# Where the list products of a graph-attention layer stand in TensorE's order, and when its last masks are loaded

## The chip, the core and the metric

The program runs on one core of a Trainium2 chip, in one launch. A core has five engines with an instruction queue each: PE (TensorE, matrix products), DVE (VectorE), ACT (ScalarE), POOL (GpSimd, here the issuer of gathers) and SP (SyncE, the issuer of most other transfers). All transfers are moved by the core's 16 DMA engines. The metric is the device time of the launch in microseconds (us).

## What is computed

Four layers over one graph of N = 2708 nodes with D = 512 features. Each layer is `x = layernorm(x + layer(x, adj))`. Layers 0, 1 and 3 multiply the adjacency with features and the features with weights. The change lies in layer 2, which holds two attention sub-layers one after the other:

```
def _gat_layer(x, W, adj):
    proj = x @ W
    Wh, Ws = jnp.split(proj, 2, axis=-1)
    scores = Wh @ Ws.T
    a = jax.nn.softmax(scores, axis=-1) * adj
    out = a @ Wh
    out = out + x
    return jax.nn.leaky_relu(out, NEG_SLOPE)
```

The softmax runs over all 2708 scores of a row before the adjacency masks them. The adjacency is sparse (about 0.6% of its entries are set), and the kernel uses that: the product `a @ Wh` is not made densely, but over lists of the neighbours that a block of 128 nodes has.

## The kernel before

**Chunks and walks.** The rows of the score matrix are split into six chunks of 512, 512, 512, 512, 384 and 276 columns (`CH`; chunk 0 to 5). The scores are kept transposed, so a chunk is 22 tiles (`NB`) of 128 nodes by the chunk's width. `Attention.layer` runs over the chunks. In *walk* k PE computes the scores of chunk k: products into `spx`, `spy` and `sp`, for the chunks of 384 columns and more in a form with seven products instead of eight on half tiles. ACT copies them out of PSUM, and DVE keeps the running maximum `top`.

**Softening.** In the same walk k DVE and ACT *soften* chunk k-1 (`soften`, called by `layer` between the steps of the walk): subtract the shift, exponentiate (ACT), add to the sum, multiply with the mask `a` of the adjacency, and store the tile to a DRAM table `pairs`, by SP. Beside each row of softened scores the table holds the row of features `Wh` (stored earlier from `z`). The masks are loaded in six groups of up to four tiles (`load_mask`, by SP): groups 0 and 1 at the walk's first two steps, group g+2 when the softening comes to group g. The last chunk is softened after the last walk.

**Lists.** When a chunk has been softened, POOL gathers rows of `pairs` by index lists (`fetch`, rows `g<-pairs,givers`), each 128 rows into a tile of a ring of 11 (`WIDES`). PE multiplies a gathered tile's scores with its features (`weigh`, rows `acc<-g`). For each block of 128 nodes there are 12 gathers: four lists that are full 128x128 products and eight quarter lists, 128x32, issued four together. A chunk of 512 columns has 48 gathers, the sixth has 27; both sub-layers together have 510. The lists of chunk k are gathered and multiplied from walk k+2 on; what is left when the walks end follows in the *tail*.

**The order of the work.** No scheduler reorders: `issue` (L71) records every instruction with a dependency on the one before it on its engine, so each engine runs in the order in which Python issues, and every row of the profile carries L71. Where list products stand among PE's products is decided at build time by a clock of the kernel's own, `self.clock`, which is advanced by what the issued products should take (`cost`). A gather is given a time (`fetch`): it begins when the one before it is done, takes 1.15 us, and its tile is taken as there 6 us later; for the first gather of a chunk the begin is put at the clock + 16. `weigh` issues the next list product if its tile is there by that clock, and returns False if not. `fetch_ahead` issues gathers up to 10 ahead (`AHEAD`) of the products. `layer` calls `weigh` up to three times after each step ("end") of a walk; at a step's middle ("mid") it only softens. With `wait=True` the product is issued whatever the clock says.

**The tail.** After the walks the softening of the last chunk and the remaining lists are mixed with other PE work that a generator, `fill`, hands out step by step: for the first sub-layer `second` (the mixing and projection of the second), for the second sub-layer `early`, the first products of layer 3 (`acc<-m,xh` and `acc<-m,xl`). `early` needs normalized rows of the attention's result, and calls `need`, which issues list products with `wait=True` until those rows are made: all of chunk 3 and one block and four lists of chunk 4.

A walk's stretch of the second sub-layer is named by W and its number; W5 is the start of walk 5 there, 1888.9 us.

Of the kernel before, what the change touches and what calls it, by code (L numbers as in the profile page):

```python
# [22 lines left out]
NB = 22  # L23
NP = NB * P
DC = D // P
# [24 lines left out]
def rows_of(i):  # L50
    return min(P, N - i * P)
# [434 lines left out]


STREAMED = 4
SOFT = NB + 2 * 2
ALONE = 18  # L490
SEVEN = [k for k in range(len(CH)) if CH[k][1] >= 384]
# [884 lines left out]
class Chunk:  # L1376


    def __init__(self, ly, k):
        self.ly, self.k, self.cw = ly, k, CH[k][1]  # L1380
        self.name = f"{ly.number}_{k}"
        self.blocks = blocks_of(k)
        self.s, self.masks, self.ends = {}, {}, []
        self.half = self.cw // 2
        self.seven = k in SEVEN
        self.part, self.complete, self.ready, self.top = {}, [], [], None
        self.softened = 0
        self.apart = 2 if self.seven else 1
        self.fetched, self.rden = [], None
        self.x, self.first = {}, {}  # L1390
        self.rows = set()
        self.mv = None

        self.to_weigh = []
        for q, (i, _, _) in enumerate(self.blocks):
            ts = lists_of(i)
            self.to_weigh += [(q, t, t is ts[0], t is ts[-1]) for t in ts]
        self.to_fetch = [(q, t) for q, ts, _, _ in self.to_weigh for t in ts]
        self.first_fetch = self.to_fetch[0]
# [9 lines left out]
class Attention:  # L1409
# [7 lines left out]
    def __init__(self, fast):  # L1417
        self.f, self.k, self.nc = fast, fast.k, fast.nc
        self.page, self.bank = fast.page, fast.bank
        tc = self.k.tc  # L1420
        self.scratch = self.k.ctx.enter_context(
            tc.tile_pool(name="pairs", bufs=1, space=DRAM)
        )

        self.pairs = [
            [
                self.scratch.tile([NP, 2 * PAIR + D], FP, tag=f"p{a}{b}", name=f"pairs{a}{b}")
                for b in range(2)  # L1430
            ]
            for a in range(2)
        ]
        self.mixed = self.scratch.tile([DC, P, D], FP, tag="mixed", name="mixed")
        self.quarter = [
            [
                self.scratch.tile(
                    [2, P, pairs_of(k)[0] * P], FP, tag=f"q{a}_{k}", name=f"quarter{a}_{k}"
                )
                for k in range(len(CH))  # L1440
            ]
            for a in range(2)
        ]
        self.sums = [
            [
                self.scratch.tile([3, P, 2, 2 * P], FP, tag=f"u{a}_{k}", name=f"sums{a}_{k}")
                for k in range(STREAMED)
            ]
            for a in range(2)
        ]  # L1450
        self.layers = [AttentionLayer(a, self.pairs[a]) for a in range(2)]
        self.clock, self.fetch_free, self.pending = 0.0, 0.0, []
        self.left = None


    def blank(self):
# [140 lines left out]
    def sum_weights(self, ly, k):  # L1597
# [6 lines left out]
        names = ("s1", "s2", "s4")  # L1604
        if k < STREAMED:
            ly.streamed[k] = [self.page(f"{n}_{a}_{k}", FP, (P, 2, wide)) for n in names]
# [273 lines left out]
    def soften(self, ch):  # L1880


        nc, v, cw = self.nc, ch.softened, ch.cw
        ch.softened += 1
        if v < NB:
            n = rows_of(v)
            s = ch.s[v][:n, :cw]
            nc.vector.tensor_sub(s, s, ch.shift[:n, :cw])
        j = v - ch.apart
        if 0 <= j < NB:  # L1890
            s = ch.s[j][: rows_of(j), :cw]
            nc.scalar.activation(s, s, AF.Exp)
        j -= ch.apart
        if j < 0:
            return
        if j == NB - 1:
            ch.softened = SOFT
        if j == 0 and ch.k >= 2:
            while self.chunks[ch.k - 2].to_fetch:
                self.weigh(True)  # L1900
        if j % DC == 0 and j + 2 * DC < NB:
            self.load_mask(ch, j // DC + 2)
        n = rows_of(j)
        s = ch.s[j][:n, :cw]
        if j == 0:
            ch.sum = self.page(f"sum{ch.name}")
            nc.vector.tensor_copy(ch.sum[:, :cw], s)
        else:
            nc.vector.tensor_add(ch.sum[:n, :cw], ch.sum[:n, :cw], s)
        nc.vector.tensor_mul(s, s, ch.masks.pop(j)[:n, :cw])  # L1910
        to = ch.ly.pairs[ch.k % 2][j * P : j * P + n, :]
        if cw == BANK:
            nc.sync.dma_start(
                to[:, : 2 * PAIR].rearrange("j (r x) -> j r x", x=PAIR)[:, :, D:],
                ch.s[j][:n, :].rearrange("j (r x) -> j r x", x=2 * P),
            )
            return
        for r in range(2):
            w = min(2 * P, cw - r * 2 * P)
            nc.sync.dma_start(  # L1920
                to[:, r * PAIR + D : r * PAIR + D + w],
                ch.s[j][:n, r * 2 * P : r * 2 * P + w],
            )
# [17 lines left out]
    def fetch(self, ch):  # L1941


        q, t = ch.to_fetch.pop(0)
        g = self.f.wide(f"g{ch.name}_{q}_{t}")
        i, _, w = ch.blocks[q]

        for b in (q, q + 1):
            self.load_rows(ch, b)

        h = t // ONLY if t < QUARTERS * ONLY else (QUARTERS - 1, 0)[q % 2]
        first, width = (D + P + h * QW, D + P - h * QW) if q % 2 else (0, D + (h + 1) * QW)
        self.nc.gpsimd.indirect_dma_start(
            out=g[:, :width],
            out_offset=None,
            in_=ch.ly.pairs[ch.k % 2][:, :],
            in_offset=bass.IndirectOffsetOnAxis(ap=self.k.givers[:, i, t : t + 1], axis=0),
            element_offset=(q // 2) * PAIR + first,
        )

        begin = max(self.fetch_free, self.clock + (16 if (q, t) == ch.first_fetch else 0))
        self.fetch_free = begin + 1.15
        ch.fetched.append((g, self.fetch_free + 6))

# [28 lines left out]
    def weigh(self, wait=False):  # L1993

        nc = self.nc
        self.fetch_ahead()
        ch = next((c for c in self.chunks if c.to_weigh), None)
        if ch is None:
            return False
        q, ts, first, last = ch.to_weigh[0]  # L2000
        if len(ch.fetched) < len(ts):
            return False
        if ch.fetched[len(ts) - 1][1] > self.clock and not wait:
            return False
        ch.to_weigh.pop(0)
        if ch.rden is None:
            self.divisor(ch)
        w = ch.blocks[q][2]
        gs = [ch.fetched.pop(0)[0] for _ in ts]
        if first:  # L2010
            ch.acc = self.bank(1, f"acc{ch.name}_{q}")
            if ch.ly.number == 1:
                ch.first[q] = self.page(f"x1{ch.name}_{q}")
                self.nc.sync.dma_start(ch.first[q][:w], self.k.saved[1][ch.blocks[q][0]][:w])
        for h, g in enumerate(gs):
            lo, m = (0, w) if len(gs) == 1 else (h * QW, QW)
            e, z = (0, P - lo) if q % 2 else (D + lo, 0)
            nc.tensor.matmul(
                ch.acc[lo : lo + m],
                g[:, e : e + m],  # L2020
                g[:, z : z + D],
                start=first,
                stop=last,
            )
        self.advance(cost(D) if len(gs) == 1 else 1.1)
        if last:
            a = (ch, q, ch.acc, ch.x.pop(q), ch.first.pop(q, None))
            self.later(1.5, lambda: self.end(*a))
        self.fetch_ahead()
        return True  # L2030
# [86 lines left out]
    def layer(self, ly, chunks, fill):  # L2117
        f = self.f
        self.chunks, self.made = chunks, {}
        for k, ch in enumerate(chunks):  # L2120
            old = chunks[k - 1] if k else None
            following = chunks[k + 1] if k + 1 < len(chunks) else None

            n = -1
            for what in self.walk(ch):
                if what == "mid":
                    if old and n >= 3 and old.softened < SOFT:
                        self.soften(old)
                    continue
                n += 1  # L2130
                if old and n < 2:
                    self.load_mask(old, n)
                    self.greatest(old, last=n == 1)
                if old and n >= 4:
                    for _ in range(n % 2 == 0 if ch.seven else 1 + n % 2):
# [15 lines left out]
                        self.restore(ly, i)  # L2151
                self.greatest(ch)

                for _ in range(3):
                    if not self.weigh():
                        break
                if old and n == 2:
                    self.shift_rows(old)
                if old and n == 3:
                    self.shift_columns(old)  # L2160
            assert not old or old.softened == SOFT
        last = chunks[-1]
        self.load_mask(last, 0)
        self.load_mask(last, 1)
        self.greatest(last, last=True)
        self.until(self.clock + 3, fill)
        self.shift_rows(last)
# [119 lines left out]
```

## Time and profile before

| what | us |
| --- | --- |
| median of three runs | 2363.23 (2360.31 to 2371.82) |
| the profiled execution | 2341.13 |
| its span (first to last instruction) | 2339.0, mean granted clock 0.985 |

The windows of the profile, cut by stage, for the attention layer: the stage's length, the busy time of the engines in it, PE's granted clock, and the share of time in which the DMA engines are busy.

| stage (us from the span's start) | length | PE | DVE | POOL | clock | DMA |
| --- | --- | --- | --- | --- | --- | --- |
| sub-layer 0, walk 2 (900 to 1000) | 100 | 92.0 | 79.5 | 51.2 | 0.95 | 0.82 |
| walk 3 (1000 to 1105) | 105 | 99.9 | 81.6 | 49.5 | 0.98 | 0.79 |
| walk 4 (1105 to 1184) | 79 | 74.7 | 65.7 | 40.7 | 0.96 | 0.84 |
| walk 5 (1184 to 1247) | 63 | 61.9 | 52.2 | 39.2 | 1.00 | 0.98 |
| tail (1247 to 1467) | 220 | 214.2 | 69.5 | 84.1 | 0.98 | 0.96 |
| sub-layer 1, walk 2 (1605 to 1710) | 105 | 97.5 | 90.0 | 53.2 | 0.97 | 0.81 |
| walk 3 (1710 to 1813) | 103 | 95.1 | 86.2 | 50.7 | 0.98 | 0.81 |
| walk 4 (1813 to 1889) | 76 | 69.8 | 68.0 | 44.0 | 1.00 | 0.90 |
| walk 5 (1889 to 1949) | 60 | 58.6 | 51.2 | 36.3 | 1.00 | 0.90 |
| tail up to the last forced list (1949 to 2026) | 77 | 52.3 | 32.1 | 41.1 | 0.87 | 0.84 |
| the rest, with layer 3 (2026 to 2339) | 313 | 298.8 | 132.8 | 61.4 | 0.99 | 0.41 |

How to read it: a stage in which PE's busy time falls short of its length holds waits of PE. A clock below 1.00 means that PE ran part of the stage at half speed; that time counts as busy. POOL's busy time is that of issuing gathers. The rows quoted further on have the start, the length, the engine, the line, the operation, output and inputs, the count, and in brackets the idle time of the engine just before with what ended it ("issue": nothing that the profile shows).

### The profile page before, as it was taken

What the parts mean: (1) busy time and instruction counts of PE and PEld (TensorE: products, weight loads), DVE (VectorE), ACT (ScalarE), POOL (GpSimd) and SP (SyncE); (2) the same over time, 40 slices, a digit from 0 to 9 for tenths busy, and PEclk for the clock granted to TensorE, in tenths of its full rate; (3) what the DMA queues carried; (4) which work ended last, traced back from release to release, by engine and by line L of the source; (5) the groups of instructions that cost most, each with busy time, mean ns of one, the idle gap of its engine ahead of it and who ended that gap; (6) DMA issues with size and microseconds to landing.
All of it is one profiled execution on the core that took longest, in us unless ns stands there. A gap on an engine that the chain in (4) does not pass through costs nothing.

```text
span 2339.0 us, 29486 instructions
## 1 busy us (share of the span) xinstructions
PE 2237.2 (96%) x9724; PEld 1515.8 (65%) x9724; DVE 1547.5 (66%) x3180; ACT 725.9 (31%) x1654; POOL 717.8 (31%) x827
## 2 busy tenths in 40 slices
PE   9999999999999998999999999998998997899997
PEld 6776876777545786566764345787565763466685
DVE  6777787777655679778784512579888896354523
ACT  7444452222111243233332101243233332251221
POOL 2433521111000002635566450002634564643000
PEclk9999999999999999999999999999999998999999
DMA  9966752223576426968899998426978899884311
GB/s 346 283 186 189 205 148 76 79 77 115 194 262 253 157 77 205 335 218 318 293 362 360 341 399 333 169 78 210 330 243 286 307 306 343 265 249 148 110 47 42
DMA packets 285139, 523.27 MB, mean 224 GB/s; under 512 B 42926, under 2 KB 134758, under 8 KB 284976
## 3 DMA queue, kind: packets, MB, share of 16 engines
q1 hardware_dynamic: 216320, 306.34, 37.9%
q0 software_dynamic: 68656, 214.96, 27.6%
q8 instruction: 78, 1.28, 0.2%
q14 instruction: 85, 0.70, 0.1%
HBM read 335.34 MB, written 185.83 MB: 223 GB/s over the span
## 4 chain that ended last, share of the span: by engine, by line
PE 71%; DVE 13%; issue 6%; DMA 6%; ACT 2%; POOL 1%; SPq 1%; another core or an unknown queue 0%; DVEq 0%; ACTq 0%; POOLq 0%
PE acc L71 27%; PE spx L71 10%; PE mm L71 8%; PE spy L71 8%; PE z L71 6%; PE wst L71 6%; DVE s L71 5%; PE sp L71 3%; DVE sum L71 2%; DMA at<-in_adj_t 1%; DVE top L71 1%; DMA g<-pairs,givers 1%; DMA x<-in_x 1%; DMA x<-x 1%; DVE r L71 1%
## 5 line engine op out<-in xcount | busy, mean ns | idle before, releaser
L71 POOL DMA_INDIRECT g<-pairs,givers x510 | 535.8, 1051 | 912.5 <-issue 359.3
L71 PE MATMUL acc<-m,xh 128*128 128x512 f32 (+4 forms) x1584 | 566.1, 379 | 8.4 <-issue 7.0
L71 PE MATMUL acc<-m,xl 128*128 128x512 f32 (+4 forms) x1584 | 549.5, 365 | 11.0 <-DVE xl L71 9.4
L71 PEld LDWEIGHTS acc<-m,xh 128*128 128x128 f32 (+1 forms) x1584 | 288.1, 188 | 71.9 <-issue 28.6
L71 PEld LDWEIGHTS acc<-m,xl 128*128 128x128 f32 (+1 forms) x1584 | 288.3, 188 | 54.7 <-DVE xl L71 10.4
L71 PE MATMUL acc<-g 128*32 128x512 f32 (+1 forms) x1020 | 285.0, 610 | 12.2 <-DMA g<-pairs,givers 7.5
L71 PE MATMUL mm<-w,ht 128*128 128x512 f32 (+1 forms) x528 | 223.3, 593 | 0.0
L71 ACT CAST m<-at 128x512 fp32r<-128x512 uint8 (+5 forms) x396 | 199.1, 567 | 40.2 <-DMA at<-mask 20.1
L71 PE MATMUL spx<-xs,wst_sb 128*128 128x256 f32 (+1 forms) x800 | 201.3, 375 | 9.2 <-DVE s L71 9.1
L71 PEld LDWEIGHTS spx<-xs,wst_sb 128*128 128x128 f32 x800 | 149.3, 193 | 47.2 <-issue 14.8
L71 DVE TENSOR_TENSOR s<-s,shift 128x512 f32<-128x512 f32 (+3 forms) x264 | 162.4, 619 | 24.7 <-ACT shift L71 14.4
L71 ACT ACTIVATE s<-s 128x512 f32<-128x512 f32 (+3 forms) x264 | 152.0, 582 | 84.8 <-DVE s L71 74.7
L71 DVE TENSOR_TENSOR s<-s,a 128x512 f32<-128x512 f32 (+3 forms) x264 | 166.0, 629 | 18.5 <-issue 9.5
L71 PEld LDWEIGHTS acc<-g 128*32 128x32 f32 (+1 forms) x1020 | 79.7, 136 | 148.5 <-issue 107.4
L71 PEld LDWEIGHTS mm<-w,ht 128*128 128x128 f32 (+1 forms) x528 | 95.8, 186 | 116.6 <-issue 112.3
L71 ACT COPY s<-spx 128x256 f32<-128x256 f32 (+1 forms) x300 | 106.0, 361 | 196.0 <-PE spx L71 143.5
L71 DVE TENSOR_TENSOR sum<-sum,s 128x512 f32<-128x512 f32 (+4 forms) x252 | 156.3, 620 | 4.1 <-ACT s L71 4.1
L71 DVE TENSOR_TENSOR top<-top,s 128x512 f32<-128x512 f32 (+4 forms) x240 | 149.6, 623 | 13.7 <-ACT s L71 9.6
L71 PE MATMUL z<-w,xt 128*128 128x512 f32 (+1 forms) x352 | 151.4, 596 | 0.0
L71 PE MATMUL wst<-xt,mixed 128*128 128x512 f32 (+2 forms) x384 | 150.9, 545 | 0.0
L71 PE MATMUL spy<-xs,wst_sb 128*128 128x256 f32 (+1 forms) x480 | 121.9, 377 | 9.4 <-DVE s L71 9.2
L71 PE MATMUL sp<-xs,wst_sb 128*128 128x276 f32 (+5 forms) x512 | 129.1, 460 | 0.0
(190 smaller groups left out, 2686.3 us busy)
## 6 DMA issues: line engine op xcount, KB each, us to landing
pairs<-z_sb SPq DMA_DIRECT2D x84, 768.0 KB
pairs<-s SPq DMA_DIRECT2D x168, 256.0 KB
s<-sums SPq DMA_DIRECT2D x96, 256.0 KB
at<-in_adj_t SPq DMA_DIRECT2D x84, 256.0 KB
xres<-x POOLq DMA_DIRECT2D x44, 256.0 KB
x<-o POOLq DMA_DIRECT2D x43, 256.0 KB
pairs<-s SPq DMA_DIRECT2D x84, 128.0 KB
a<-mask SPq DMA_DIRECT2D x40, 256.0 KB
```

Of the source, the lines that this page charges most:

```text
L71: ins = call(*args, **kw)
```

## The change

Five edits, all of order; what is computed stays the same.

- `FIRST_LANDS`: the build-time clock puts the first gather of a chunk at the clock + 5 instead of + 16.
- `SPACING`: in walks 2, 3 and 4 a list product is issued only once the clock has reached `next_list`, which then moves on by 1.2 or 1.1 us per list (from no earlier than the clock - 4). In these walks `weigh` is called up to two times after a step instead of three.
- `weigh` is also called once at every "mid" of a walk, in all walks.
- `masks_ahead`: for chunks 4 and 5 five mask groups are loaded ahead of the softening instead of two; those of chunk 4 at the first five steps of walk 5.
- The first masks of chunk 5 (five groups) are loaded at the last five steps of walk 5, and no longer (two groups) after it.

The ring, `AHEAD` and the instructions stay as they are. In the order of the instructions as built, list products of chunks 0 and 1 begin earlier in their walks; all 48 of chunk 2 stand in walk 4 (before: 32 there and 16 in walk 5); 40 of chunk 3 stand in walk 5 (before: 20); and in the tail of the second sub-layer some 26 lists follow walk 5 up to what `early` needs (before: 44), and the lists of chunk 5 stand earlier among the products of layer 3.

```diff
--- before.py
+++ after.py
@@ -486,6 +486,8 @@
 
 
 STREAMED = 4
+FIRST_LANDS = 5
+SPACING = {2: 1.2, 3: 1.2, 4: 1.1}
 SOFT = NB + 2 * 2
 ALONE = 18
 SEVEN = [k for k in range(len(CH)) if CH[k][1] >= 384]
@@ -1385,6 +1387,7 @@
         self.seven = k in SEVEN
         self.part, self.complete, self.ready, self.top = {}, [], [], None
         self.softened = 0
+        self.masks_ahead = 2 if k < STREAMED else 5
         self.apart = 2 if self.seven else 1
         self.fetched, self.rden = [], None
         self.x, self.first = {}, {}
@@ -1451,6 +1454,7 @@
         self.layers = [AttentionLayer(a, self.pairs[a]) for a in range(2)]
         self.clock, self.fetch_free, self.pending = 0.0, 0.0, []
         self.left = None
+        self.spacing, self.next_list = 0.0, 0.0
 
 
     def blank(self):
@@ -1898,8 +1902,8 @@
         if j == 0 and ch.k >= 2:
             while self.chunks[ch.k - 2].to_fetch:
                 self.weigh(True)
-        if j % DC == 0 and j + 2 * DC < NB:
-            self.load_mask(ch, j // DC + 2)
+        if j % DC == 0 and j + ch.masks_ahead * DC < NB:
+            self.load_mask(ch, j // DC + ch.masks_ahead)
         n = rows_of(j)
         s = ch.s[j][:n, :cw]
         if j == 0:
@@ -1958,7 +1962,7 @@
             element_offset=(q // 2) * PAIR + first,
         )
 
-        begin = max(self.fetch_free, self.clock + (16 if (q, t) == ch.first_fetch else 0))
+        begin = max(self.fetch_free, self.clock + (FIRST_LANDS if (q, t) == ch.first_fetch else 0))
         self.fetch_free = begin + 1.15
         ch.fetched.append((g, self.fetch_free + 6))
 
@@ -2002,6 +2006,10 @@
             return False
         if ch.fetched[len(ts) - 1][1] > self.clock and not wait:
             return False
+        if self.spacing and not wait:
+            if self.clock < self.next_list:
+                return False
+            self.next_list = max(self.next_list, self.clock - 4) + self.spacing * len(ts)
         ch.to_weigh.pop(0)
         if ch.rden is None:
             self.divisor(ch)
@@ -2122,14 +2130,19 @@
             following = chunks[k + 1] if k + 1 < len(chunks) else None
 
             n = -1
+            self.spacing = SPACING.get(k, 0.0)
             for what in self.walk(ch):
                 if what == "mid":
                     if old and n >= 3 and old.softened < SOFT:
                         self.soften(old)
+                    self.weigh()
                     continue
                 n += 1
+                if old and n < old.masks_ahead:
+                    self.load_mask(old, n)
+                if not following and n > NB - 1 - ch.masks_ahead:
+                    self.load_mask(ch, n - NB + ch.masks_ahead)
                 if old and n < 2:
-                    self.load_mask(old, n)
                     self.greatest(old, last=n == 1)
                 if old and n >= 4:
                     for _ in range(n % 2 == 0 if ch.seven else 1 + n % 2):
@@ -2151,7 +2164,7 @@
                         self.restore(ly, i)
                 self.greatest(ch)
 
-                for _ in range(3):
+                for _ in range(2 if self.spacing else 3):
                     if not self.weigh():
                         break
                 if old and n == 2:
@@ -2159,9 +2172,8 @@
                 if old and n == 3:
                     self.shift_columns(old)
             assert not old or old.softened == SOFT
+        self.spacing = 0.0
         last = chunks[-1]
-        self.load_mask(last, 0)
-        self.load_mask(last, 1)
         self.greatest(last, last=True)
         self.until(self.clock + 3, fill)
         self.shift_rows(last)
```

## A prediction, made from the kernel before

> **What bounds the kernel now.** I read the page first, then the chain of waits, the windows of the second attention sub-layer's end, and its timelines by engine.
>
> ```profile
> span 2339.0 us, 29486 instructions
> PE 2237.2 (96%) x9724; PEld 1515.8 (65%) x9724; DVE 1547.5 (66%) x3180; ACT 725.9 (31%) x1654; POOL 717.8 (31%) x827
> PE 71%; DVE 13%; issue 6%; DMA 6%; ACT 2%; POOL 1%; SPq 1%; another core or an unknown queue 0%; DVEq 0%; ACTq 0%; POOLq 0%
> L71 POOL DMA_INDIRECT g<-pairs,givers x510 | 535.8, 1051 | 912.5 <-issue 359.3
> L71 PE MATMUL acc<-g 128*32 128x512 f32 (+1 forms) x1020 | 285.0, 610 | 12.2 <-DMA g<-pairs,givers 7.5
> ```
>
> PE bounds the program: 96% busy, and most of the chain is its own work. No instruction is taken away, so a gain can only come from PE's 102 idle us, from time in which it is busy but slowed by its clock, and from list products that run poorly. The 7.5 us put down to gathers understate the last: a product that waits for its gather piece by piece counts as busy.
>
> ```profile
> 1920.00:1960.00 40.00, 30.73 (x130) 19.54 (x128) 30.46 (x68) 17.50 (x41) 22.64 (x20) 0.91 0.91 325
> 1960.00:2000.00 40.00, 31.26 (x92) 12.17 (x93) 17.97 (x36) 5.90 (x10) 18.41 (x20) 0.87 0.88 315
> 2000.00:2040.00 40.00, 33.34 (x102) 16.58 (x101) 13.74 (x29) 7.68 (x15) 26.11 (x24) 0.96 0.79 252
> ```
>
> In these windows (busy us and counts of PE, PEld, DVE, ACT, POOL, then clock, DMA share, GB/s) PE loses 25 of 120 us and its clock falls to 0.87: the worst stretch of the program. The timeline says why:
>
> ```profile
> 1940.66 0.32 SPq L71 DMA_DIRECT2D a<-mask  x1
> 1953.34 0.56 DVE L71 TENSOR_TENSOR s<-s,a 128x384 f32<-128x384 f32 x1 [7.50 <-issue]
> 1956.91 0.80 PE L71 MATMUL acc<-m,xh 128*128 128x512 f32 x1 [6.97 <-issue]
> 1966.94 0.79 PE L71 MATMUL acc<-m,xl 128*128 128x512 f32 x1 [9.24 <-DVE xl L71]
> 1975.59 0.95 POOL L71 DMA_INDIRECT g<-pairs,givers  x1 [18.99 <-PE acc L71]
> ...
> 1981.32 5.48 PE L71 MATMUL acc<-g 128*32 128x512 f32 x14
> ...
> 2018.94 1.05 PE L71 MATMUL acc<-g 128*32 128x512 f32 x2 [2.37 <-DMA g<-pairs,givers]
> 2020.85 5.39 PE L71 MATMUL acc<-g 128*128 128x512 f32 x8 [0.86 <-DMA g<-pairs,givers]
> 2025.67 0.79 PE L71 MATMUL acc<-m,xh 128*128 128x512 f32 x1
> ```
>
> A mask load of chunk 4 was issued 12.6 us before its multiplication could start; DVE stood 7.5 us. Behind it in DVE's queue were the rest of that softening and the `xl` splits, so PE idled 6.97 and 9.24 us; POOL, whose ring of 11 tiles empties only when PE multiplies, stood 18.99 us. Then 36 lists came as one burst, 1981.32 to 2025.67: 44.4 us, at POOL's pace of 0.95 + 0.30 = 1.26 us a gather. I call 2025.67 the marker; walk 5 (the scores of the last chunk) began at 1888.9, so the marker is W5+136.8.
>
> **What the Trainium skill says.** "TensorE: Matmul & The Clock Gate", Part 1, What's actually happening: after an idle window of some 3.4 us PE runs at half clock until a busy window has passed. The trace agrees: 17.1 us at 0.5 from 1953.1, 3.4 to 6.8 us after most gaps. An idle of 3 us costs about 1.7 us more. The same page, Part 2, Step-by-step: matmuls stay in program order, only weight loads are pulled ahead. So a list product ordered ahead of its gather's landing blocks all scores behind it; the burst shows it. "DMA: Bandwidth & Descriptors", Issuing engines are not separate DMA queues: SP's and POOL's transfers interleave on the same 16 DMA engines. The trace has these 79 to 91% busy in the windows above, and gathers landing 4 to 6 us after issue, a mask after 12.6. So denser gathers may land later.
>
> **The change part by part.** PE, DVE, ACT, POOL and SP have the same instructions in both programs as built; only order moves. I lay PE's changed order over the times of before.
>
> *Masks five groups ahead.* Chunk 4's loads leave their places between SP's stores of `s` (each 0.45 to 0.5 us of issue) for the start of walk 5; chunk 5's are issued in walk 5 too. Five loads ahead of SP's stores delay these by 5 x 0.35, under 2 us, at a time when stores of chunk 4 have not begun. The 7.5 us on DVE go. PE's 16.2 us do not go whole: the softening of chunk 4 is late next, and `xl` stands behind it. I leave PE 5 us there: -11 us, clock windows apart.
>
> *Lists of chunk 2 all in walk 4.* Before, 32 of 48 were there and 16 in walk 5, so the first gather of chunk 3 came at 1901.5 (W5+12.6). Now it can come by about W5+4. The 16 lists cost walk 4 what they leave walk 5: 16 x 0.47 = 7.5 us (12 lists that are ready take 4 x 0.87 + 2 x 1.07 = 5.6 us, or 0.47 each). No gain by itself.
>
> *Lists of chunk 3 and the end of sub-layer 1.* The spread over "mid" points puts 40 instead of 20 of chunk 3's lists into walk 5, so POOL's ring empties there and its 18.99 us stop goes; the burst shrinks from 36 to some 26 lists. From walk 5's start to the marker POOL must issue 48 + 16 = 64 gathers. At 1.28 to 1.4 us (what it does while unblocked and in practice) that is 82 to 90 us; with the start at W5+4 and a landing of 6 us the marker is W5+92 to W5+100. PE's own work in the stretch (136.8 less 16.2 of idle, about 9 of half clock, and the burst's 44.4 against 36 x 0.47 = 17) gives 84; less the 7.5 moved to walk 4 still leaves gathers as the limit. I take W5+96: 136.8 - 96 = 41 us earlier, less 7.5 paid in walk 4: **-33 us**; the mask's 11 are within it, since POOL was stopped at the same time. Bounds -15 (pace 1.6) and -40.
>
> *Lists of chunk 5.* `FIRST_LANDS` 5 instead of 16 makes the build clock believe in an early landing. Before, its first list product came at marker + 74.6 (2100.3) with the gathers from 2080.5. In the changed order it stands after 19 groups of 1.82 us and 20 lists at 0.47, marker + 44, while DVE's softening of chunk 5 (2041.3 to 2068.2), 44 stores on SP and the landing come to marker + 50 when eight softening steps go ahead of the `xl` wait of 7.07 us. PE would stand about 6 us; bounds 0 and 14: **+6 us**.
>
> *Walks 2 to 4 of both sub-layers.* Their PE gaps over 0.3 us sum to 17 us in sub-layer 0 and 14 in sub-layer 1; half-clock windows add (20.4 + 10.2)/2 = 15. Two of them:
>
> ```profile
> 910.82 1.13 PE L71 MATMUL spx<-xs,wst_sb 128*128 128x256 f32 x4 [3.83 <-DVE s L71]
> 1024.75 2.08 PE L71 MATMUL spy<-xs,s 128*128 128x256 f32 x4 [3.38 <-issue]
> ```
>
> At 1024.75 scores alone had outrun the engines that empty their banks; a list product there (the changed order has the first at about 1022) gives PE other work. At 910.82 no list is ready, so it stays. Even spacing (1.2 us of build clock a list) should also stop clumps in which POOL waits at 11 ahead (6 to 19 us idle after the eleventh gather of each chunk). Of 46 us I count those near 1024, 1124 and 1809, halved: **-8 us**. Bounds -25, and +10 from gathers not landed: the first list would be wanted at 919.4 (landing 917), 1022 (1014), 1126 (1115), 1621 (1620), 1724 (1716), so slack is 1 to 11 us.
>
> *End of sub-layer 0.* Chunk 4's first list moves ahead of the `z` work; 5.83 us idle at 1306.31 plus 6.8 us at half clock, 9.2 in all, can go, but its gathers (first at 1278.1, POOL stopped 16.5 us at 1293.5) are then wanted earlier. I take **-3 us**, between -9 and +8.
>
> Sum: -33 + 6 - 8 - 3 = -38 us. The profiled execution took 2341.13 us (span 2339.0), so 2303. The runs' median 2363.23 lies 22.1 us above it; with the same offset 2325.
>
> **The rivals.** *Tail only*: gaps at walk starts belong to the DVE and ACT chain of maxima and shifts (3.83 at 910.82 is such), and lists fill none. For it: the releasers named; against: the idle at 1024.75 with gathers landed. -38 + 8 = -30: 2333. *The gathers are the bound*: with DMA near 0.9, pace becomes 1.55 us, 64 x 1.55 + 10 = W5+109, -28 + 7.5 = -20; chunk 5 +10; the walks 0: 2353. Against it, POOL kept 1.26 us beside a DMA share of 0.88. *Only the mask is mended*: the burst stays since chunk 4's gathers wait for its stores: -5 to -11, about 2355. Against it: those stores were all issued by 1969.3, and chunk 3's gathers alone need till W5+68. *Slower: lists ahead of their landing.* One mechanism at each of 12 chunk starts: PE's order takes the first lists before the gathers are there, 3 us of idle and 1.7 of half clock, 4.7 x 12 = +56, against the tail's -30: +26, 2389. It decides from 3.2 us per start on (38/12), that is when landing takes 4 to 5 us more than before where slack is 1. For it: the slack of 1 us at 919 and 1621; against: 8 to 11 at the others, and before's waits for gathers in the walks are all under 1 us (0.40 at 975.01).
>
> **How the numbers follow.** Forecast 0.50; tail only 0.20; gathers as bound 0.15, half of it within 0.5% (11.8 us, about what a measurement of this kernel can tell from no change); mask only 0.05, within it; slower 0.10. So faster 0.78, same 0.12, slower 0.10. The range goes from -66 (tail -40, chunk 5 at 0, walks -20, sub-layer 0 -6) to the bound by gathers and some us over it, -4: 2297 to 2359.
>
> **What would show it.** No DVE idle over 1 us ahead of a masked multiplication in walk 5; POOL without a stop of over 8 us between W5 and the marker; the marker at W5+90 to +102; chunk 5's first list behind a wait of some us; fewer half-clock windows in walks 3 and 4. I am wrong if PE shows idle ahead of the first `acc<-g` of most chunks, if mean gather pace passes 1.5 us, or if walks 2 to 4 grow by more than the 7.5 us that walk 4 is given.

## The result, and the profile after

Over 20 runs each on one chip the changed kernel took 2377.11 us in the median (2368.28 to 2386.34), the kernel before 2356.71: a ratio of 1.0085, 95% interval 1.0068 to 1.0102. It is slower by some 20 us, where 38 us faster had been forecast. Two more measurements of the same pair, on other chips, gave 1.0117 (1.0071 to 1.0164) and 1.0070 (1.0050 to 1.0090). The ratios here and further on leave out one run of the experiment e1 (9387 us, at a granted clock of 0.227) and four runs of the kernel before that were over 1.5% above its fastest.

The page of the changed kernel has, against the lines of before: more time of PE and more idle time around it, and in the row of list products a wait for gathers that grew from 7.5 to 23.6 us. (The two profiled executions are further apart than the kernels: 2341 us is 16 below the median of before, 2386 is 9 above that of the changed kernel.)

```profile
span 2384.2 us, 29431 instructions
PE 2260.4 (95%) x9724; PEld 1521.3 (64%) x9724; DVE 1551.4 (65%) x3180; ACT 722.7 (30%) x1654; POOL 710.8 (30%) x827
PE 74%; DVE 12%; DMA 5%; issue 4%; another core or an unknown queue 2%; POOL 1%; ACT 1%; SPq 1%; POOLq 0%; DVEq 0%; ACTq 0%
L71 POOL DMA_INDIRECT g<-pairs,givers x510 | 529.1, 1037 | 937.4 <-DMA pairs<-s 369.7
L71 PE MATMUL acc<-g 128*32 128x512 f32 (+1 forms) x1020 | 295.8, 622 | 26.2 <-DMA g<-pairs,givers 23.6
```

PE has the same 9724 products and is busy 23 us longer: part of that is half clock. POOL's idle time before gathers reads differently too. By the list of waits, what is ended by PE freeing the ring (`acc`) fell from 216.5 to 68.7 us, and what is ended by stores of softened scores (`pairs<-s`) grew from 213.1 to 369.7 (37 us of it in the one long wait between the sub-layers). The gathers wait for the softening more than before.

For the stages a second profile of the kernel before was taken, because the one shown ahead of the prediction (2341.13 us) lay some 16 us under its kernel's median. The second (span 2364.7) and one of the changed kernel (span 2372.6), taken on the same chip, are each within 6 us of their medians there. (Outside these stages the changed kernel's profile came out 10 us shorter, in work that the change does not touch.) One profile of a stage is no sharp measure: in the third stage below the kernel before took 282.6 us in its first profile, on another chip, and 298.4 in this one; the changed kernel took 300.2 and 304.8. The windows are cut where PE transposes a chunk's maxima, which it does once in each walk. First line: walks 2 to 4 of sub-layer 0; second: its walk 5 and tail; third: walks 2 to 4 of sub-layer 1; fourth: its walk 5, the tail, and layer 3 to the end. Columns are the length, then busy us and counts of PE, PEld, DVE, ACT, POOL, then clock, DMA share and GB/s. Before:

```profile
921.20:1205.50 284.30, 267.56 (x1229) 190.45 (x1228) 221.70 (x379) 91.67 (x229) 145.27 (x140) 0.97 0.84 294
1205.50:1550.80 345.30, 341.08 (x1212) 188.06 (x1211) 153.63 (x324) 68.75 (x163) 113.76 (x113) 1.00 0.84 305
1627.80:1926.10 298.30, 267.79 (x1197) 188.50 (x1196) 243.09 (x432) 92.30 (x227) 148.41 (x140) 0.95 0.81 282
1926.10:2364.70 438.60, 399.59 (x1656) 260.98 (x1654) 205.52 (x458) 119.13 (x257) 129.02 (x140) 0.96 0.53 177
```

After:

```profile
912.50:1200.90 288.40, 268.52 (x1245) 185.82 (x1244) 223.10 (x382) 91.07 (x229) 147.79 (x145) 0.98 0.88 299
1200.90:1564.60 363.70, 347.44 (x1195) 189.62 (x1194) 153.23 (x322) 67.57 (x163) 112.68 (x110) 0.98 0.80 284
1640.00:1944.80 304.80, 273.52 (x1213) 186.59 (x1211) 247.63 (x439) 93.90 (x230) 148.12 (x144) 0.96 0.82 284
1944.80:2372.60 427.80, 394.28 (x1639) 262.90 (x1639) 203.00 (x453) 117.37 (x254) 127.88 (x138) 0.96 0.52 177
```

Walks 2 to 4 took in 8 more lists per sub-layer (16 more products), worth 4 us at 0.47 us a list, and the stage behind them lost as many. So the first line is level, the third is 2 us worse (less than that stage differs between profiles of one kernel), the fourth 7 us better, and the second is the loss: 18.4 us longer although it has 8 lists less to do. Its PE idles 16.3 us where it idled 4.2, and runs some of it at half clock (0.98 against 1.00).

The timeline of the changed kernel (same profile) shows the two places in that tail:

```profile
1281.51 1.14 POOL L71 DMA_INDIRECT g<-pairs,givers  x1 [7.94 <-DVE xr L71]
1285.76 1.10 PE L71 MATMUL acc<-g 128*128 128x512 f32 x2 [1.27 <-DMA g<-pairs,givers]
1287.17 3.53 PE L71 MATMUL acc<-g 128*128 128x512 f32 x4 [0.32 <-DMA g<-pairs,givers]
1292.21 1.13 PE L71 MATMUL acc<-g 128*128 128x512 f32 x2 [1.50 <-DMA g<-pairs,givers]
...
1346.05 1.11 POOL L71 DMA_INDIRECT g<-pairs,givers  x1 [9.72 <-DMA pairs<-z_sb]
...
1353.17 2.05 PE L71 MATMUL acc<-g 128*128 128x512 f32 x2 [4.25 <-DMA g<-pairs,givers]
1355.69 4.26 PE L71 MATMUL acc<-g 128*128 128x512 f32 x6 [0.47 <-DMA g<-pairs,givers]
```

1281.51 and 1346.05 are the first gathers of chunks 4 and 5; PE stands at their first lists, 4 and 7 us later. The two products of the list at 1353.17 take 2.05 us where those at 1285.76 take 1.10, and four take 3.53 at 1287.17: the granted clock is 0.5 for 3.4 us from 1286.9 and for 6.8 us from 1351.8. Waits for gathers sum to 7.8 us in this stage, and to nothing over 0.2 us in the profile of before taken beside it. There the first gather of chunk 4 and its first list stand so (timeline):

```profile
1292.65 0.95 POOL L71 DMA_INDIRECT g<-pairs,givers  x1 [0.30 <-issue]
...
1318.24 1.96 PE L71 MATMUL acc<-g 128*128 128x512 f32 x4
```

The list stood 19 us behind its gather's landing (by the last of the gather's DMA packets). Walk 5 began at 1194.67 in both profiles, so the times compare directly: in the changed kernel the gather is issued 11 us earlier than this, but its list stands 32 us earlier.

### The profile page after: what moved, and what is told of

It reads as the page before. It is cut to its first block, busy times and chain, and to the rows that moved or that the text cites. A ratio compares the mean times of both kernels' runs of the same rounds, so it can differ in the third digit from the quotient of the medians.

```text
span 2384.2 us, 29431 instructions
## 1 busy us (share of the span) xinstructions
PE 2260.4 (95%) x9724; PEld 1521.3 (64%) x9724; DVE 1551.4 (65%) x3180; ACT 722.7 (30%) x1654; POOL 710.8 (30%) x827
## 4 chain that ended last, share of the span: by engine, by line
PE 74%; DVE 12%; DMA 5%; issue 4%; another core or an unknown queue 2%; POOL 1%; ACT 1%; SPq 1%; POOLq 0%; DVEq 0%; ACTq 0%
PE acc L71 31%; PE spx L71 9%; PE mm L71 8%; PE spy L71 7%; PE z L71 6%; PE wst L71 6%; DVE s L71 4%; PE sp L71 3%; DMA g<-pairs,givers 2%; DVE sum L71 2%; DVE top L71 1%; DVE r L71 1%; PE mix L71 1%; DMA at<-in_adj_t 1%
## 5 line engine op out<-in xcount | busy, mean ns | idle before, releaser
L71 POOL DMA_INDIRECT g<-pairs,givers x510 | 529.1, 1037 | 937.4 <-DMA pairs<-s 369.7
L71 PE MATMUL acc<-g 128*32 128x512 f32 (+1 forms) x1020 | 295.8, 622 | 26.2 <-DMA g<-pairs,givers 23.6
L71 PE MATMUL sp<-xs,wst_sb 128*128 128x276 f32 (+5 forms) x512 | 134.6, 482 | 1.2 <-issue 1.1
```

What stands on the lines that cost most here:

```text
L71: ins = call(*args, **kw)
```

## Experiments

Theory A: list products spread singly among the scores hold up PE, ACT and DVE in the walks. Theory B: with `FIRST_LANDS` 5 the first lists of a chunk are ordered ahead of their gathers. Theory C: the early mask loads are in the way. Four groups of kernels ran, each on one chip with the kernel before beside it. The chips differ: the kernel before took 2293.89, 2360.43, 2364.27 and 2293.48 us in the four groups. So ratios are compared, and stages between profiles of the same group or of the two chips at 2293; where other profiles are set side by side, it is said. The changed kernel itself did not run on a chip at 2293.

| group | kernel | median us | ratio to before (95%) |
| --- | --- | --- | --- |
| 1 | e1: + 16 | 2283.27 | 0.9952 (0.9937 to 0.9968) |
| 1 | e2: no spacing | 2329.70 | 1.0166 (1.0131 to 1.0201) |
| 1 | e3: no middles | 2303.48 | 1.0043 (1.0025 to 1.0060) |
| 1 | e4: masks alone | 2289.58 | 0.9979 (0.9965 to 0.9993) |
| 2 | changed kernel | 2377.26 | 1.0117 (1.0071 to 1.0164) |
| 2 | e5: + 16, no middles | 2346.99 | 0.9957 (0.9935 to 0.9978) |
| 2 | e6: + 5 alone | 2364.29 | 1.0025 (1.0005 to 1.0046) |
| 2 | e7: + 16 for chunks 4, 5 | 2358.06 | 1.0003 (0.9982 to 1.0023) |
| 3 | kernel before | 2366.34 | 0.9988 (0.9965 to 1.0011) |
| 3 | changed kernel | 2378.33 | 1.0070 (1.0050 to 1.0090) |
| 3 | e8: + 5 for three late chunks, else + 16, no middles | 2323.54 | 0.9810 (0.9759 to 0.9861) |
| 3 | e9: + 10 | 2338.00 | 0.9884 (0.9837 to 0.9932) |
| 4 | e10: + 16 in sub-layer 0 | 2299.89 | 1.0032 (1.0019 to 1.0044) |
| 4 | e11: + 10, no middles | 2273.16 | 0.9903 (0.9872 to 0.9934) |
| 4 | e12: + 10 and + 5, no middles | 2274.36 | 0.9917 (0.9884 to 0.9949) |

The lengths of the four stages in the profiles of the two chips at 2293 (one profile each), where e1 and e10, whose first sub-layer is the same program, agree within 1 us:

| kernel | walks 2-4, sub-layer 0 | its W5 and tail | walks 2-4, sub-layer 1 | the rest |
| --- | --- | --- | --- | --- |
| e4: masks alone, + 16 | 259.0 | 337.4 | 267.4 | 428.7 |
| e1: + 16, spacing, middles | 261.2 | 336.2 | 265.6 | 424.5 |
| e10: + 16, then + 5 | 262.2 | 336.2 | 282.1 | 420.8 |
| e3: + 5, no middles | 257.0 | 355.9 | 276.7 | 413.2 |
| e2: + 5, middles, no spacing | 268.3 | 354.4 | 284.5 | 425.9 |
| e11: + 10, no middles | 257.0 | 336.8 | 266.9 | 415.2 |
| e12: + 10 and + 5, no middles | 255.5 | 337.6 | 271.1 | 408.5 |

### e1: the first gather at + 16 again

```diff
-FIRST_LANDS = 5
+FIRST_LANDS = 16
```

> The changed kernel with the first gather of each chunk put at the build clock + 16 again, all else as changed. Theory A (lists spread singly among the score products hold up the hand-over between PE, ACT and DVE in the walks) expects little: within 6 us of the changed kernel, so some 14 to 26 us above the kernel before. Theory B (with FIRST_LANDS 5 the first list products stand ahead of their gathers' landing; PE's waits for gathers grew from 7.5 to 23.6 us) expects 10 us or more less than the changed kernel, so 0 to 10 us above the kernel before, and gather waits back under 12 us. Theory C (the early mask loads are in the way) expects no change against the changed kernel.

It is 0.48% faster than before. The rest of the change is a gain of some 11 us, and the one number turns it into a loss. PE's waits for gathers are 5.3 us in this profile. That is what theory B expects; theory C falls. (The comparison with the changed kernel is one across chips; e9 below makes it on one chip.)

### e2: no spacing, and e3: no products at the middles

```diff
-SPACING = {2: 1.2, 3: 1.2, 4: 1.1}
+SPACING = {}
```

> The changed kernel without the spacing in walks 2 to 4 (and so with up to three list products after a step again), all else as changed. Theory A expects the walks 2 to 4 to return to their length before: 12 to 20 us less than the changed kernel, 0 to 8 us above the kernel before. Theories B and C expect it within 6 us of the changed kernel, some 20 us above the kernel before.

```diff
                         self.soften(old)
-                    self.weigh()
                     continue
```

> The changed kernel without the list products at the middle of a step, all else as changed. Theory A expects a part of the loss back, 5 to 15 us less than the changed kernel, since lists then stand only between steps. Theories B and C expect it within 6 us of the changed kernel.

e2 went against all theories: 1.66% slower, where the changed kernel's three ratios are 1.0070 to 1.0117 (the intervals overlap, and the chips differ). So the even spacing is no burden and seems to be a help: with + 5 and without spacing, walks 2 to 4 are the longest of the table in both sub-layers (268.3 and 284.5). Theory A, by which they would return to their length before, falls for the spacing. e3 is 0.43% slower than before, less than any measurement of the changed kernel, as theory A had it for the middles; what they cost is told by e10 below. In e3 the tail of sub-layer 0 is 19.7 us longer than in e1, and 14.6 us of it are PE's waits for gathers (e1: none over 0.2 us each in that tail).

e3 also shows one wait of a kind that the prediction had not looked for, at the end of walk 2 of sub-layer 1 (timeline, ACT and PE):

```profile
1696.36 0.20 ACT L71 ACTIVATE rs_t<-rs_v 128x4 f32<-128x4 f32 x1 [8.40 <-DVE rs_v L71]
1696.47 0.35 ACT L71 COPY s<-spy 128x256 f32<-128x256 f32 x1
1696.88 2.07 PE L71 MATMUL spy<-xs,wst_sb 128*128 128x256 f32 x4 [6.84 <-ACT s L71]
```

The lists of a chunk end earlier, so (a reading of the order, not an experiment) its layernorm's small ACT step comes earlier in ACT's queue; it waits for a DVE that is busy with the softening, and the copies that PE needs wait behind it. "TensorE: Matmul & The Clock Gate", Part 1, Architectural detail, of the Trainium skill has ACT's and DVE's queues as strict first in, first out; the trace agrees: ACT's copy of `s` starts 0.11 us after the step that waited 8.40 us.

### e4: the masks alone

```diff
-        if j % DC == 0 and j + 2 * DC < NB:
-            self.load_mask(ch, j // DC + 2)
+        if j % DC == 0 and j + ch.masks_ahead * DC < NB:
+            self.load_mask(ch, j // DC + ch.masks_ahead)
...
-        self.load_mask(last, 0)
-        self.load_mask(last, 1)
```

> The kernel before with the mask loads of the changed kernel and nothing else. The prediction's step says the 7.5 us stall of DVE at the end of walk 5 goes and PE's 16.2 us before layer 3 shrink to about 5: 5 to 11 us faster than the kernel before. Theory C expects it 5 us or more slower. Theories A and B expect a gain or nothing.

0.21% faster (0.07 to 0.35%), 4.3 us between the medians: a gain, just under what the step had expected. DVE's stall is gone, but PE then waits longer in one place for what DVE does next (timeline of e4):

```profile
1921.32 0.79 PE L71 MATMUL acc<-m,xl 128*128 128x512 f32 x1 [11.59 <-DVE xl L71]
```

In the profile ahead of the prediction these were 6.97 and 9.24 us; 16.2 became 11.6. By these two profiles, which are of different chips, the 7.5 us saved on DVE shortened PE's wait by 4.6.

### The changed kernel beside e5, e6 and e7

> The changed kernel itself on the chip of the next three, as the value that they are held against. Its first measured ratio was 1.0085. If the parts add up on every chip, it stands 15 to 25 us above the kernel before; from the four runs so far (with FIRST_LANDS 16 it was 0.5% faster than before, without the middles 0.4% slower) theory B expects it here too between 0.7 and 1.2% slower.

> FIRST_LANDS 16 and no list products at the middle of a step; spacing and masks as changed. If the loss from FIRST_LANDS and that from the middles add up, it is 0.6 to 1.0% faster than before (the 0.5% of FIRST_LANDS 16 with middles and a part of the 0.4% that the middles cost beside FIRST_LANDS 5). If the middles cost only where lists stand close to their gathers' landing, or if they are what brings more of chunk 3 into walk 5, it is between 0.2 and 0.5% faster.

```diff
-        begin = max(self.fetch_free, self.clock + (16 if (q, t) == ch.first_fetch else 0))
+        begin = max(self.fetch_free, self.clock + (5 if (q, t) == ch.first_fetch else 0))
```

> The kernel before with the first gather of each chunk put at the clock + 5, and nothing else. Theory B (this number alone makes the loss) expects 15 us or more slower than before, with PE waiting for the first gathers of chunks 4 and 5 in the tail of the first sub-layer (7.0 and 5.8 us where it was seen). If the number hurts only together with the early masks, which stand on SP ahead of the last stores of chunk 4, it is within 8 us of the kernel before.

```diff
-        begin = max(self.fetch_free, self.clock + (FIRST_LANDS if (q, t) == ch.first_fetch else 0))
+        begin = max(self.fetch_free, self.clock + ((FIRST_LANDS if ch.k < STREAMED else 16) if (q, t) == ch.first_fetch else 0))
```

> The changed kernel with + 16 for chunks 4 and 5 alone and + 5 for chunks 0 to 3. Theory B in its narrow form (the loss sits at the first lists of the last two chunks, whose stores and gathers come late) expects the tail of the first sub-layer back at its length before: 12 to 22 us less than the changed kernel, so from 0.1% faster to 0.5% slower than before. If instead the loss sits in walks 2 to 4 (ACT and DVE chains meeting lists that start and end earlier), it stays within 6 us of the changed kernel.

e7 goes from the changed kernel's 1.0117 to 1.0003, 19 us between the medians, by moving only the first lists of chunks 4 and 5. Its tail of sub-layer 0 is back at 351.0 us in the windows, from 362.4 in the changed kernel's profile of this group. That is theory B in its narrow form. e6 is the kernel before with + 5 alone, without early masks: its tail of sub-layer 0 is 360.8 us, as long as the changed kernel's, so this loss needs neither masks, spacing nor middles. But its whole loss is only 0.25%, 4 us, where theory B had expected 15 or more. A part of the answer is its end of sub-layer 1, 421.6 us, against 438.6 and 439.1 in the two profiles of before (other chips). Why the changed kernel loses 13 us more than e6 stays open: the profile of e6 is its slowest run of 20 and that of the changed kernel its fastest of 4, so their stages can't tell. By the ratios e5 is as fast as e1: at + 16 the middles neither cost nor bring anything that could be measured.

### e8 and e9: less of it, and later

> The kernel before, unchanged, for a second profile: on the first chips its one profile took 2341 us where the median of its runs was 2357 to 2360, so its stages may read some 20 us short in all. Both theories expect a ratio of 1.00. If the profile of before was a fast draw, its stages come out longer here and the changed kernel's first sub-layer walks 2 to 4 differ by less than the 9 to 11 us seen so far.

> The changed kernel on the chip of the next two. From the two ratios so far (1.0085 and 1.0117) between 0.7 and 1.2% slower than before, by the stages: the tail of sub-layer 0 longer by 15 to 20 us, walks 2 to 4 of sub-layer 1 longer by 8 to 16, the tail of sub-layer 1 shorter by 8 to 16.

```diff
-        begin = max(self.fetch_free, self.clock + (FIRST_LANDS if (q, t) == ch.first_fetch else 0))
+        begin = max(self.fetch_free, self.clock + ((FIRST_LANDS if ch.ly.number == 1 and ch.k in (2, 3, 4) else 16) if (q, t) == ch.first_fetch else 0))
...
-                    self.weigh()
```

> Spacing and masks as changed, no list products at the middles, and the first gather at + 5 only for chunks 2, 3 and 4 of the second sub-layer, + 16 elsewhere. If the stages add up, the tail of sub-layer 0 and walks 2 and 3 of sub-layer 1 keep the length that they have with + 16, and the tail of sub-layer 1 keeps its gain of 10 to 16 us: 0.7 to 1.2% faster than before, the fastest of all. If the gain in that tail is only work pushed into walk 4 and given back there, it is no better than + 16 everywhere: 0.4 to 0.5% faster.

```diff
-FIRST_LANDS = 5
+FIRST_LANDS = 10
```

> The changed kernel with FIRST_LANDS 10. With + 16 the first lists of the last two chunks of sub-layer 0 stood 17 to 24 us behind their gathers' landing, with + 5 at it, with PE idle. If the loss is a matter of this slack running out, + 10 still has some left there: no wait over 1.5 us for a first gather in that tail, and the time between 0.2 and 0.8% faster than before. If the loss grows with every us by which lists stand earlier, it is about half way: between 0.1% faster and 0.6% slower.

The changed kernel did as expected but for walks 2 to 4 of sub-layer 1, which came out 6.4 us longer and not 8 to 16. e8 is 1.9% faster than before and e9 with + 10 everywhere 1.16%, both more than expected (0.7 to 1.2, and 0.2 to 0.8). e9 and the changed kernel ran on one chip and differ in the one number alone: 2338.00 against 2378.33 us. The windows of e9, sub-layer 0's walk 5 and tail, and the rest after walk 4 of sub-layer 1:

```profile
1208.50:1552.90 344.40, 338.15 (x1195) 188.53 (x1194) 153.22 (x323) 67.59 (x163) 110.14 (x109) 1.00 0.82 299
...
1919.30:2335.00 415.70, 389.77 (x1640) 258.84 (x1638) 204.47 (x457) 118.84 (x257) 128.97 (x136) 0.99 0.52 181
```

The tail has the lists of the changed kernel (1195 products) and none of its 18 us; the end keeps more than the changed kernel's gain (427.8). So the cost is a matter of slack that runs out, not of lists standing earlier as such: in e9 the first list of chunk 4 stood 13 us behind its gather's landing, in the changed kernel 0.5. The number is not worth the tail alone: beside its 19 us, e9's walks 2 to 4 of sub-layer 1 are 15 us shorter than the changed kernel's (289.4 against 304.8), its end 12 and its walks 2 to 4 of sub-layer 0 3 us.

### e10, e11 and e12: the second sub-layer, and the middles

```diff
-        begin = max(self.fetch_free, self.clock + (FIRST_LANDS if (q, t) == ch.first_fetch else 0))
+        begin = max(self.fetch_free, self.clock + ((FIRST_LANDS if ch.ly.number == 1 else 16) if (q, t) == ch.first_fetch else 0))
```

> The changed kernel with the first gather at + 16 in the first sub-layer and + 5 in the second. If the tail of sub-layer 0 is the whole loss, its W5 and tail return to 345 to 351 us (from 362 to 364) and the kernel is faster than before by what the second sub-layer gains: 0 to 0.6%. If walks 2 to 4 of sub-layer 1 carry a part of 10 us or more, it is 0 to 0.5% slower than before.

> FIRST_LANDS 10, spacing and masks as changed, no list products at the middles. If the middles cost only where lists have no slack, it stands within 0.25% of the run with + 10 and middles, 1.0 to 1.4% faster than before. If they cost of themselves, it is 1.4 to 1.9% faster.

> As the one before, with + 5 for chunks 2, 3 and 4 of the second sub-layer. The fastest so far had this with + 16 elsewhere and was 1.9% faster than before. If + 10 is also better than + 16 in the first sub-layer's tail and in walks 2 and 3, this is 2.0 to 2.5% faster; if not, 1.6 to 2.0%.

e10 tells where another part of the loss is. The tail of sub-layer 0 is healed (336.2), and the kernel is still 0.32% slower than before. Against e1, of which it differs by + 5 in sub-layer 1 alone, walks 2 to 4 there are 16.5 us longer, 2 of them for four more lists. The windows of walk 2 of sub-layer 1 show how. e1 (the first and the last two sixths or so of the walk):

```profile
1596.00:1612.00 16.00, 15.77 (x78) 13.32 (x78) 13.09 (x22) 6.46 (x16) 8.71 (x10) 1.00 0.86 323
...
1660.00:1676.00 16.00, 15.04 (x66) 9.73 (x65) 15.55 (x28) 5.55 (x13) 3.18 (x4) 1.00 0.85 323
1676.00:1690.00 14.00, 12.87 (x54) 8.52 (x53) 13.25 (x30) 3.99 (x10) 5.06 (x5) 1.00 0.56 177
```

e10:

```profile
1590.00:1606.00 16.00, 15.90 (x77) 11.21 (x74) 7.93 (x14) 4.10 (x10) 12.34 (x13) 1.00 0.98 368
...
1654.00:1670.00 16.00, 14.97 (x72) 11.82 (x72) 15.48 (x31) 9.62 (x20) 0.00 (x0) 1.00 0.45 144
1670.00:1691.00 21.00, 16.59 (x63) 10.83 (x62) 20.15 (x38) 4.24 (x11) 3.73 (x4) 0.92 0.71 231
```

In the first 16 us of the walk PE is as busy in both, but in e10 with 8 lists where e1 has one, so with fewer scores; DVE, whose work follows from the scores, has 7.93 us of work instead of 13.09. In the second half of e1's walk (from 1628) DVE is 95 to 98% busy. In e10, at the end, when e10's lists are used up, DVE is at 96% and PE waits for it: 16.59 busy of 21. So PE bounds the first part of such a walk (no idle in e1 from 1612 to 1660) and DVE the last: over the six windows DVE has the same work (85.6 us in e1, 86.5 in e10), and idles 6 us more in e10. The walk is 6.7 us longer (94.9 against 101.6 from one transpose to the next). In walks 3 and 4 PE's waits for DVE at the scores and at the transposes of the maxima are 10.3 us in e10 and 2.5 in e1. This is not a wait at a list, which is why the row of list products does not show it. The account is read from two traces; no run changed DVE's work alone.

The middles: e3 and e10 differ in sub-layer 1 by them alone, 276.7 + 413.2 against 282.1 + 420.8: 13 us with + 5. With + 10, e11 (0.97% faster without them) and e9 (1.16% with them) cannot be told apart. e12 is no better than e11: 0.83% faster, where 1.6% or more had been expected from e8's 1.9%, so what made e8 as fast as that did not come back on this chip, and why stays open. By the ratio on its own chip the best version is e8, then e9, e11 and e12. The interval of e8 overlaps with that of e9 and not with the other two, and e8 and e12 were not run side by side.

## Why the prediction was wrong

- **End of sub-layer 0, "-3 us, between -9 and +8".** Measured +18.4 with 8 lists fewer. This is the step that failed most. Its text saw that the gathers "are then wanted earlier", and left that to the upper bound of +8: the step looked at chunk 4 alone, left out that `FIRST_LANDS` does the same to chunk 5 there, and laid the new order over old times in which DVE and SP have long finished. They had not. The last masked multiplication of chunk 4 (timelines of the second profile of before, then of the changed kernel) comes 11 us later, though walk 5 begins at 1194.67 in both:

```profile
1257.94 0.55 DVE L71 TENSOR_TENSOR s<-s,a 20x384 f32<-20x384 f32 x1
1269.30 0.55 DVE L71 TENSOR_TENSOR s<-s,a 20x384 f32<-20x384 f32 x1
```

In the first profile of before the first lists of chunks 4 and 5 stood 23 and 18 us behind their gathers' landing, in the second 19 and 10. This slack was a good that the old number had bought for both chunks; + 5 spent all of it: 0.5 and 0.7 us are left.

- **The rival "slower: lists ahead of their landing"** had the mechanism. Its number of places was too high: not 12 starts but four, those of chunks 4 and 5 of both sub-layers, where PE waits 4.33, 3.12, 3.68 and 3.66 us in the first profile after. In the tail of sub-layer 0 its price was too low, some 10 us at each of two starts and not 4.7. Its deciding point was wrong: it wanted gathers that land 4 to 5 us later than before. The first gathers of chunks 4 and 5 there land 4 to 7 us after their issue in both profiles of before and in all three of the changed kernel. They were even issued earlier than before, behind stores of a softening that ran late; the lists moved forward by more.
- **Walks 2 to 4, "-8 us".** Measured level in sub-layer 0 and +2 in sub-layer 1 (with the extra lists taken off); on the chips at 2293 + 5 alone costs 14 there (e10 against e1). The step asked what PE would do at the gaps and put no price on DVE, which the page has at 66% of the span. In the walks 2 to 4 of sub-layer 1 DVE was 84 to 90% busy before (the table of stages); by the windows of e1 and e10 it was the second bound, and the lists took its input away. One reading was off as well: PE's gaps over 0.3 us in these walks sum to 21 us and not to 14 (the table of stages has PE busy 262 of 284 us). And half clock came after less idle than the rule that the prediction cites: 3.4 us at 0.5 began at 1286.9 in the changed kernel, when PE by its records had been busy 2.1 of the 3.4 us before. The measurement decides.
- **Chunk 3 and the end of sub-layer 1, "-33 us".** With chunk 5's "+6" that made -27; measured -10.8 in the windows, of which 4 are lists moved away. POOL's stop did go, and the burst did shrink. What failed is "gathers as the limit", W5+96: the last forced list began at W5+110. The chain was that of chunk 4's softening (timeline of the changed kernel: last masked multiplication on DVE, last stores on SP, first gather, first list):

```profile
2011.44 0.55 DVE L71 TENSOR_TENSOR s<-s,a 20x384 f32<-20x384 f32 x1
...
2015.14 2.34 SPq L71 DMA_DIRECT2D pairs<-s  x2
...
2020.71 0.95 POOL L71 DMA_INDIRECT g<-pairs,givers  x1 [6.39 <-DMA xr<-y]
...
2027.93 2.05 PE L71 MATMUL acc<-g 128*128 128x512 f32 x2 [1.58 <-issue]
2030.31 16.09 PE L71 MATMUL acc<-g 128*128 128x512 f32 x30 [0.33 <-issue]
```

Walk 5 began at 1935.2, so the softening ended at W5+77, where it ended before (76.9; W5+71 and W5+73 in the other two profiles of the changed kernel). The mask stall (6.2 us in the profile of before beside it) is gone, but DVE has 4 us more work in this stretch, 63.9 against 59.8, and walk 5 has some 38 lists instead of 34. From there 16 us pass to the first list, and 17 more to the last of the 16 that are forced, which follow each other at the pace of their gathers. This is what the rival "only the mask is mended" had said of the burst: chunk 4's gathers wait for its stores.

- **Masks.** Right in kind: no masked multiplication of chunks 4 and 5 has over 1 us of DVE idle ahead of it in the three profiles of the changed kernel (the line at 2011.44 has no bracket). The part alone brought 4.3 us, just under the 5 to 11 of the rival that counted on it.
- **Chunk 5 in layer 3, "about 6 us".** Right in kind: PE waits 3.66 us at its first list in the first profile after, 4.86 in the second, and 4.80 in e10.

Adding up: +22 in the tail of sub-layer 0 and +2 in the walks, -7 at the end, each with the moved lists taken off, make +17; the runs of that group say +14 between the medians, so the stages hold the loss within what single profiles can tell. The forecast had put -3 - 8 - 27 = -38 in the same places.

## What to carry over

A number in a scheduler's own clock that looks like a guess of a latency can be the slack for everything that the clock does not model; here it counted PE's work only, and the + 16 held DVE's softening and SP's stores. Before such a number is cut, list for each place where it acts what really ends last there, and price the places one by one. And when work of the busiest engine is moved forward, ask which engine lives on the work that is pushed back: an engine at 66% of the span can be the bound of the stage.

## What was not expected of the hardware

The same kernel before took 2293 us on two chips (groups 1 and 4) and 2357 to 2364 in the other measurements, 3% apart. In one thing the profiles differ plainly: by the records of the slower chips, other engines see PE's results late. In the first profile after, walk 4 of sub-layer 1 (timeline):

```profile
1884.33 0.81 PE L71 MATMUL spy<-t,s 128*128 128x192 f32 x4
...
1891.88 0.32 ACT L71 COPY s<-spy 128x192 f32<-128x192 f32 x1 [7.10 <-remote]
1892.25 1.27 PE L71 MATMUL spy<-xs,s 128*128 128x192 f32 x3 [4.15 <-ACT s L71]
```

By its record the product into `spy` ended at 1885.14, yet ACT, whose copy waits for PE's semaphore alone, copied it at 1891.88, at the time of a batch of eight semaphore updates of PE that the trace has 0.05 us apart. Count as such a batch four or more updates of PE, each at most 0.07 us behind the one before it, after more than 1.3 us without any. Between 830 and 2140 us the trace has 31 of them after, 18 in the first profile before, 18 to 26 in profiles of groups 2 and 3, and none or one in those of groups 1 and 4. They occur only while gathers and list products run. What causes them stays open; the traces of the slower chips also lack some 8 to 15% of the updates that the products should make. They are there with and without the change, and + 5 costs time on chips without them too (e2, e3, e10), so they do not explain what + 5 costs.
